# A block of four experts placed behind the wide pairs, five narrow pairs kept on the chip, and gathered rows added one pair sooner

## The chip, the cores and the metric

The kernel runs on one core of a Trainium2 chip. A core has five engines that run side by side, each through its own fixed list of instructions, in order: TensorE (PE) for matmuls and transposes, VectorE (DVE), ScalarE (ACT), GpSimd (POOL) and SyncE (SP). They wait for one another through semaphores. ACT, POOL and SP also issue transfers between the core's memory and the memory outside of it, which 16 DMA engines carry out. The metric is the time of one execution in microseconds (us) as the device counts it; less is better.

## The reference

One layer with three parts, in float32, on 256 tokens of 512 numbers: an attention block, a state-space block with a convolution, and a mixture of experts. The change touches the third part alone:

```python
scores = jax.nn.sigmoid(x @ gate_w)              # 256 tokens, 32 experts
topk_w, topk_i = jax.lax.top_k(scores, 6)
topk_w = topk_w / (jnp.sum(topk_w, axis=-1, keepdims=True) + 1e-20)
combine = jnp.sum(one_hot(topk_i, 32) * topk_w[..., None], axis=1)
g = jnp.einsum('td,edf->tef', x, wg)             # wg, wu: 32 x 512 x 192
u = jnp.einsum('td,edf->tef', x, wu)
routed = jnp.einsum('tef,efd,te->td', silu(g) * u, wd, combine)
shared = silu(x @ sg) * (x @ su) @ sd
return routed + shared
```

So each token goes through 6 of 32 experts, and the results are added with the token's weights. The layer's input is added on top, as after the other parts.

## The kernel before

Tokens stand in two token tiles of 128 (NT = 2). The attention and the state-space part come first and take the span up to about 839 us. The routing then ranks the experts: the first 8 (FIXED) stand as they are, the other 24 are sorted by how many tokens chose them. Sorted experts get 128 rows each down to position 18 (WIDE), and 64 rows behind that, except the four with the fewest tokens, which get 32 rows each and share one block of 128 rows, the block of four. A second path for the case that an expert has more tokens than rows stands behind a test on the device (`crowded`); it is not taken with these inputs.

Experts go in pairs, numbered n = 0 to 15. Pairs 0 to 8 are wide (two blocks of 128 rows), the narrow pairs hold two experts in one block, and the block of four takes two numbers. The loop at L1582 walks over `units`, all pairs but the second number of the block. Before, the order is: wide pairs 0 to 8, narrow pair 9, the block of four as 10 (11 is left out), narrow pairs 12 to 15. Two constants set this: SMALL = 20 is the place at which the block of four begins, and TAIL = 8 the number of experts behind it. FOUR is the block's unit, and LAST = 16 - TAIL/2 = 12 the first unit behind it.

One pass of the loop, for unit n:

- `gate_up` (L1484 for wide pairs, L1406 for narrow ones, L1439 for the block): the gate and up products on PE into the tile `ps_egu`, SiLU on ACT into `si`, and products on DVE into `hid` (L1495, L1416, L1450). The last of them is kept as `done[n]`.
- `fetch` (L1376): rows of a later unit are gathered from `xg` into `xg_sb` by a POOL transfer. `turn` (L1387) of the next unit: PE transposes into `xgTp` (L1392), a DVE copy to `xgT` (L1394). The next `gate_up` needs that copy.
- the down products of the unit before. Up to LAST, the result goes through an ACT copy to `y_sb`, and ACT issues its write to `ye` outside the core's memory (L1520, L1472, L1466). Behind LAST, `down_here` (L1474) keeps it in `y_sb`.
- for the units kept on the chip, `spread` (L1479): matmuls (L1482) with a matrix `spread` that carries each row to its token, with its weight, adding up in the PSUM tiles `total`, one per token tile.
- `load_pair`: POOL issues the three weight transfers of the pair six places on, into the buffers that the unit before has left (L1187).
- `turn_hidden` (L1421, L1498): PE transposes `hid` into `hidTp` for the down products.

The results in `ye` come back by `gather` (L1338): six POOL transfers per token tile, one for each chosen expert of a token, into `yk` tiles, and `add` (L1348) multiplies and adds them to `x_sb` on DVE (L1351), in a chain for each token tile. Experts that are kept on the chip have no row in `ye`; the gather reads a row of zeros for them. A gather waits for all the writes to `ye` before it. Token tile 0's gathers are written at LAST and take the six buffers of the pool `yp`; token tile 1's are written one unit later and take two buffers of the ring "xg" and then four of `yp`, which come free with the adds of token tile 0. `add_behind` (L1576) writes adds that may not stand ahead of `done[n]` on DVE: three behind pair 14's, nine behind pair 15's.

The matrix `spread` is made in `weights_back` (L1540), written in the pass of unit 3: for each token tile, eight scalings on DVE (L1560) into `pick`, four transposes on PE into a tile of the ring "x" of two (L1562), which `turn` uses too, and one copy (L1563).

At the end `finish` (L1623) adds `total` to `x_sb` on DVE, and SP stores the two tiles.

The order of instructions on each engine is not just the order of the program text. The framework's planner walks through the program before launch with costs of its own: when an engine is free by its reckoning, it takes the instruction that stands first in the text among those that are ready by its reckoning. `issue_after` holds instructions back behind a given one on their engine. On the chip each engine then keeps to the list that came out, whether or not the transfers are as quick as reckoned.

Of the kernel before, what the change touches and what calls it, by code (L numbers as in the profile page):

```python
# [11 lines left out]
FP = mybir.dt.float32  # L12
# [3 lines left out]
ALU = mybir.AluOpType  # L16
# [3 lines left out]
P = 128  # L20
# [29 lines left out]
TOPK = 6  # L50
FT = FSH // P
REST = FE - P
NP = NE // 2
# [4 lines left out]
WIDE = FIXED + 10  # L58
HALFP = P // 2
QUARTER = P // 4  # L60
SMALL = 20
HEAD = 4
TAIL = 8
NPL = 2 * (NE - FIXED) + (NE - WIDE) // 2 - (NE - WIDE) + (NE - FIXED) // 2
ZROW = WIDE * P + (SMALL - WIDE) * HALFP + 4 * QUARTER
NOROOM = 2 * NE * P
# [9 lines left out]
def perceiver_layer(ctx: ExitStack, tc: tile.TileContext, a: dict, out: bass.AP):  # L76
# [64 lines left out]
    def layer(ctx, bounded):  # L141
# [1196 lines left out]
        def gather(src, rows, t, rings):  # L1338

            got = []  # L1340
            for k, (pool, tag) in enumerate(rings):
                yk = pool.tile([P, DM], FP, tag=tag, name="yk")
                G.indirect_dma_start(out=yk, out_offset=None, in_=src,
                                     in_offset=bass.IndirectOffsetOnAxis(ap=rows[:, t, k:k + 1], axis=0))
                got.append(yk)
            return got
# [175 lines left out]
        with ExitStack() as rctx:  # L1522
            main = Rounds(rctx, weights)
            yp = rctx.enter_context(tc.tile_pool(name="yp", bufs=6))
            for k in range(KD):
                ps = main.ps_x.tile([P, HEAD * P], FP, tag="x", name="ps_pick")
                for t in range(NT):
                    TE.matmul(ps, xn[:, t, k * P:(k + 1) * P], pick[:, t].rearrange("p e r -> p (e r)"),
                              start=(t == 0), stop=(t == NT - 1))
                (S.copy if k % 2 else V.tensor_copy)(picked[:, k], ps.rearrange("p (e r) -> p e r", r=P))  # L1530
            for e in range(HEAD):
                main.xgT[e // 2, e % 2] = picked[:, :, e, :]


            idx, rowf, sc, rank, mask, iota = (m[n] for n in ("idx", "rowf", "gate", "rank", "mask", "iota"))
            result_rows()

            spread, = carve(m["kv", 0], (TAIL // 2, L))

            def weights_back():  # L1540

                V.tensor_tensor(sc, sc, mask, ALU.mult)
                V.tensor_tensor(sc, sc, m["den"].unsqueeze(2).to_broadcast([P, NT, NE]), ALU.mult)

                free = NE - FIXED
                V.tensor_tensor(member, m["at"].unsqueeze(1).to_broadcast([P, TAIL, NE]),
                                iota[:, free - TAIL:free].unsqueeze(2).to_broadcast([P, TAIL, NE]), ALU.is_equal)
                of, of_all = {}, carve(members, *[(TAIL,)] * 4)
                for t in range(NT):
                    for name, v in (("rank", rank), ("sc", sc)):  # L1550
                        V.tensor_tensor(own, member, v[:, t].unsqueeze(1).to_broadcast([P, TAIL, NE]), ALU.mult)
                        of[name, t] = of_all[len(of)]
                        V.tensor_reduce(of[name, t], own, AX.X, ALU.add)
                for t in range(NT):
                    tp = main.ps_x.tile([P, TAIL // 2, P], FP, tag="x", name="spreadT")
                    for u in range(TAIL // 2):
                        w = pick[:, t, u, :]
                        for i in range(2):
                            s = 2 * u + i
                            V.tensor_scalar(w[:, i * HALFP:(i + 1) * HALFP], iota[:, 0:HALFP], of["rank", t][:, s:s + 1],  # L1560
                                            of["sc", t][:, s:s + 1], ALU.is_equal, ALU.mult)
                        TE.transpose(tp[:, u, :], w, ident)  # L1562
                    V.tensor_copy(spread[:, :, t * P:(t + 1) * P], tp)  # L1563

            FIRST, LAST, FOUR = HEAD // 2, NP - TAIL // 2, SMALL // 2
            units = [n for n in range(NP) if n != FOUR + 1]
            gate_up = lambda n: (main.gate_up if 2 * n < WIDE else main.gate_up_quarters if n == FOUR else main.gate_up_halves)(n)
            turn_hidden = lambda n: (main.turn_hidden_halves if 2 * n >= WIDE and n != FOUR else main.turn_hidden)(n)
            down = lambda n: (main.down if 2 * n < WIDE else main.down_quarters if n == FOUR else main.down_halves)(n, ye)
            def spread_last(n, tiles=range(NT)):  # L1570
                main.spread(n, spread[:, n - LAST, :], total, n == LAST, n == NP - 1, tiles)

            fetched = set()
            got, r_x, r_k = [], [(main.e4, "xg")], [(yp, "yk")]

            def add_behind(n, k0, k1):  # L1576

                with tc.issue_after(main.done[n]):
                    for k in range(k0, k1):
                        add(got[k // TOPK], k // TOPK, [k % TOPK])  # L1580

            for u, n in enumerate(units):  # L1582
                before, coming = units[u - 1], units[u + 1:]
                gate_up(n)

                for f in coming[1:3 if n == LAST else 2]:
                    if FIRST <= f and f not in fetched:
                        main.fetch(f)
                        fetched.add(f)

                if FIRST < n + 1 and coming:
                    main.turn(coming[0])
                if 0 < n <= LAST:
                    down(before)
                    if n + 1 == FIRST:
                        main.turn(n + 1)
                elif n > LAST:
                    main.down_here(before)
                if n == LAST:
                    got.append(gather(ye, row_y, 0, r_k * TOPK))  # L1600
                elif n == LAST + 1:
                    total = [main.ps_ye.tile([P, DM], FP, tag="ye", name="total") for _ in range(NT)]
                    got.append(gather(ye, row_y, 1, r_x * 2 + r_k * 4))
                if n > LAST + 1:
                    spread_last(n - 2)
                if n == NP - 2:
                    add_behind(n, 0, 3)
                if n == NP - 1:
                    add_behind(n, 3, 2 * TOPK)
                for freed in range(before, n) if n > 0 else ():  # L1610
                    load_pair(freed + NHELD)
                if n == FIRST + 1:
                    weights_back()
                    some = nc.values_load(crowded, min_val=0, max_val=1)
                turn_hidden(n)

            spread_last(NP - 2, [0])
            main.down_here(NP - 1)
            spread_last(NP - 2, [1])
            spread_last(NP - 1)  # L1620

            def finish(t):
                V.tensor_tensor(x_sb[:, t, :], total[t], x_sb[:, t, :], ALU.add)  # L1623

            def store(t):
                nc.sync.dma_start(out[t * P:(t + 1) * P, :], x_sb[:, t, :])

            with tc.If(some == 0) as arms:
                for t in range(NT):
                    finish(t)  # L1630
                    store(t)
            with arms.Else():
                for t in range(NT):
                    finish(t)
                main.weights = {}
                for n in range(NP):
                    main.weights[n] = (held[2 * (n % 2)], held[2 * (n % 2) + 1], rests[n % 2])
                    load_weights(main.weights[n], n, True)
                    for h in range(NT):
                        r0 = [(2 * n + i) * L + h * P for i in range(2)]  # L1640
                        main.fetch(n, r0)
                        main.turn(n, 2)
                        main.gate_up(n)
                        main.turn_hidden(n)
                        main.down(n, ye2, r0)

                row2f, row2 = m["m8"][:, :, 0:TOPK], row_y
                V.tensor_scalar(rowf, rowf, float(NOROOM), float(NE * L), ALU.is_lt, ALU.mult)
                V.tensor_copy(row2f, row)
                V.tensor_tensor(row2f, row2f, rowf, ALU.add)  # L1650
                V.tensor_scalar(row2f, row2f, float(NE * L), None, ALU.min)
                V.tensor_copy(row2, row2f)
                for t in range(NT):
                    add(gather(ye2, row2, t, [(main.e4, "xg")] * TOPK), t)
                    store(t)
# [55 lines left out]
```

## Time and profile before

| | |
|---|---|
| median of 3 runs | 989.08 us (988.28 to 989.34) |
| the profiled execution's own time | 982.5 us |
| its span | 980.7 us |
| PE busy in the span | 956.7 us, 98% |
| first product of the expert stage | 843.3 us into the span |
| the block of four: gate and up begin | 930.4 us |
| end of PE's last matmul | 967.7 us |
| end of the last `add` and of the last `finish` on DVE | 969.1 and 970.4 us |

All times within the execution are in us from the start of the span. Busy times add up over an engine; PE's ends are modelled, and each float32 matmul shows as two instructions, each transpose as one. In an order of time a line gives the start, the length, engine and line, the operation, output and inputs with their shapes, and in brackets how long the engine idled before it and what ended that. L numbers are lines of the kernel.

### The profile page before, as it was taken

The page shows a single profiled execution, that of the slowest core. Times are in us where ns is not written, and L with a number is a line of the kernel's source. Part 1 is how long each engine was busy: PE and PEld are TensorE (multiplying, and loading weights), DVE is VectorE, ACT ScalarE, POOL GpSimd, SP SyncE. Part 2 cuts the span into 40 slices and gives each one's busy share as a digit, 9 for nine tenths or more (in the row PEclk, how much of TensorE's full clock was granted, in tenths as well). Part 3 has the DMA queues.
Part 4 walks back from the last instruction along what each step waited for, and adds up shares of the span by engine and source line. Part 5 has one row for each costly group of instructions (what it writes and reads, how often), then busy time and mean ns, then how long its engine had stood idle before and what let it go on. Part 6 is the DMA issues. An engine that isn't in the chain of part 4 may idle for free.

```text
span 980.7 us, 8874 instructions
## 1 busy us (share of the span) xinstructions
PE 956.7 (98%) x2725; PEld 451.6 (46%) x2725; DVE 497.4 (51%) x1013; ACT 386.9 (39%) x851; POOL 203.9 (21%) x212
## 2 busy tenths in 40 slices
PE   7999999999999999999999999999999999999994
PEld 3444444444444444444444444444465655455441
DVE  4456555454454544544545445358587656622133
ACT  3645444343443434434434344353153642122220
POOL 4443002001100200200200110000014233545432
PEclk9999999999999999999999999999999999999997
DMA  9735032122313304304113121150036353899973
GB/s 329 229 75 140 35 112 106 41 44 107 86 20 131 86 1 150 76 11 150 54 33 92 64 61 32 57 168 1 0 140 218 140 174 138 308 353 358 365 303 117
DMA packets 130940, 125.12 MB, mean 128 GB/s; under 512 B 80033, under 2 KB 99266, under 8 KB 125634
## 3 DMA queue, kind: packets, MB, share of 16 engines
q1 hardware_dynamic: 119216, 77.96, 26.4%
q0 software_dynamic: 7904, 40.90, 11.4%
q10 hardware_dynamic: 3762, 5.59, 1.6%
q8 instruction: 24, 0.39, 0.2%
q14 instruction: 34, 0.28, 0.1%
HBM read 88.76 MB, written 35.67 MB: 127 GB/s over the span
## 4 chain that ended last, share of the span: by engine, by line
PE 92%; issue 2%; DVE 2%; DMA 2%; POOL 1%; ACT 1%; SPq 0%; POOLq 0%; DVEq 0%
PE scT L571 23%; PE oT L596 23%; PE ps_kv L368 17%; PE ps_egu L222 5%; PE ps_self L222 4%; PE ps_v L222 2%; PE ps_o L794 2%; PE ps_ye L1512 2%; PE ps_k L222 2%; PE ps_xbc L222 1%; PE ps_out L988 1%; DMA yk<-ye,row_y 1%; PE ps_sgu L222 1%; PE ps_ye L1515 1%; PE xgTp L1392 1%
## 5 line engine op out<-in xcount | busy, mean ns | idle before, releaser
L587 DVE TENSOR_TENSOR lacc<-lacc,prT 128x512 f32<-128x512 f32 x256 | 182.8, 715 | 239.3 <-ACT prT L577 238.6
L577 ACT ACTIVATE prT<-scT,bq,rk 128x512 f32<-128x512 f32 x256 | 198.8, 777 | 254.3 <-PE scT L571 241.8
L571 PE MATMUL scT<-qT,kT 128*128 128x512 f32 x536 | 271.6, 593 | 0.0
L596 PE MATMUL oT<-prT,v 128*128 128x512 f32 x528 | 268.3, 592 | 0.0
L571 PEld LDWEIGHTS scT<-qT,kT 128*128 128x128 f32 x536 | 101.1, 190 | 124.8 <-issue 121.7
L596 PEld LDWEIGHTS oT<-prT,v 128*128 128x128 f32 x528 | 100.2, 190 | 125.8 <-issue 115.8
L200 POOL TENSOR_TENSOR rk<-pv,mhalf 128x4 f32<-128x4 f32 x32 | 32.3, 1010 | 369.3 <-DVE pv L199 369.3
L368 PE MATMUL ps_kv<-wkv,fast 128*128 128x512 f32 x112 | 53.4, 592 | 0.0
L258 ACT ACTIVATE sq<-kraw 128x128 f32<-128x128 f32 x128 | 35.6, 278 | 45.2 <-DVE kraw L386 43.1
L368 PE MATMUL ps_kv<-wkv,ctx 128*128 128x512 f32 x112 | 52.8, 592 | 0.0
L368 PE MATMUL ps_kv<-fast,fast 128*128 128x512 f32 x112 | 52.6, 592 | 0.0
L602 DVE TENSOR_TENSOR oacc<-oT,oacc 128x512 f32<-128x512 f32 x64 | 43.7, 683 | 0.0
L368 PEld LDWEIGHTS ps_kv<-wkv,fast 128*128 128x128 f32 x112 | 21.3, 190 | 26.8 <-issue 26.8
L368 PEld LDWEIGHTS ps_kv<-fast,fast 128*128 128x128 f32 x112 | 21.3, 190 | 26.8 <-issue 21.8
L368 PEld LDWEIGHTS ps_kv<-wkv,ctx 128*128 128x128 f32 x112 | 21.3, 190 | 26.8 <-issue 23.7
L362 POOL TENSOR_TENSOR fast<-ctx 128x512 f32<-128x512 f32 x7 | 9.4, 1336 | 113.0 <-PE ps_kv L368 94.2
L386 DVE TENSOR_TENSOR kraw<-ps_kv,fast 128x256 f32<-128x256 f32 x42 | 17.8, 424 | 28.2 <-PE ps_kv L368 28.2
L1495 DVE TENSOR_TENSOR hid<-si,ps_egu 128x128 f32<-128x128 f32 x18 | 5.2, 286 | 49.4 <-ACT si L1493 49.4
L794 PE MATMUL ps_o<-wo,qT 128*128 128x512 f32 x64 | 28.8, 592 | 0.0
L222 PE MATMUL ps_self<-wq,xT 128*128 128x512 f32 x64 | 28.1, 592 | 0.0
L607 DVE RECIPROCAL lacc<-ps_l 128x512 f32<-128x512 f32 x8 | 26.8, 3349 | 0.1
L368 PE MATMUL ps_kv<-fast,ctx 128*128 128x512 f32 x56 | 26.3, 592 | 0.0
(393 smaller groups left out, 1114.8 us busy)
## 6 DMA issues: line engine op xcount, KB each, us to landing
xg<-xn SPq DMA_DIRECT2D x6, 2560.0 KB, 9.3
ctx<-in_ctxT_dram SPq DMA_DIRECT2D x7, 1024.0 KB, 5.4
kd<-tr SPq DMA_DIRECT2D x112, 64.0 KB, 2.4
kT<-kd SPq DMA_DIRECT2D x28, 256.0 KB, 2.8
ye<-y_sb ACTq DMA_DIRECT2D x20, 256.0 KB, 8.1
wq<-in_wq_dram SPq DMA_DIRECT2D x4, 1024.0 KB, 14.2
wo<-in_wo_dram SPq DMA_DIRECT2D x4, 1024.0 KB, 10.5
w_in<-in_W_inT_dram SPq DMA_DIRECT2D x4, 1024.0 KB, 5.7
```

Of the source, the lines that this page charges most:

```text
L200: return G.tensor_tensor(dst, v[:, :n], mhalf[:, :n], ALU.pow)
L222: TE.matmul(ps, lhs(k), rhs_of(k), start=(k == 0), stop=(k == KD - 1))
L258: S.activation(sq[:, h, :], raw[:, h, :], AF.Square, accum_out=ss[:, h:h + 1])
L368: TE.matmul(ps, lhs(k), rhs(k), start=(start and k == 0), stop=(k == 1), skip_group_check=True)
L571: scored.append(TE.matmul(sc, kT[:, g, i * P:(i + 1) * P], qT[:, t, heads4(g), :].rearrange("p h q -> p (h q)"), start=True, stop=True).ins)
L577: S.activation(pr, sc, AF.Exp, bias=shift, scale=SCALE if r is None else r[:, i, g:g + 1])
L587: V.tensor_tensor(la, la, pr, ALU.add)
L596: TE.matmul(outs[g, t], v[:, i, g * HD:(g + 1) * HD], pr, start=(n == 0), stop=last)
L602: V.tensor_tensor(ov, outs.pop((g, t)), ov, ALU.add)
L607: V.reciprocal(rl, ps)
L794: TE.matmul(m["ps_o", t], aT[:, t, h, :], wo[j][:, h % 4, :], start=(h == 0), stop=(h == NH - 1))
L1512: TE.matmul(ps[i], h[:, i, :], wd[i], start=True, stop=False)
```

## The change

The block of four moves one unit ahead, to directly behind the wide pairs. SMALL becomes 18 and TAIL 10, so the order is: wide pairs 0 to 8, the block of four as 9 (10 is left out), narrow pairs 11 to 15. LAST becomes 11. All five narrow pairs stand behind the block, and all of them keep their results on the chip; nineteen blocks are written to `ye` where there were twenty. `spread` has five blocks per token tile in place of four: `weights_back` makes them in two tiles of the ring "x" per token tile, four and one, and the fifth block uses the first slot of `pick` again. Token tile 0's gathers are written at unit 11 and token tile 1's at unit 12; the latter now take first four buffers of `yp` and then two of the ring "xg". At LAST the rows of three later units are fetched in place of two. Six adds are written behind pair 13's last product, four behind pair 14's and two behind pair 15's.

```diff
-SMALL = 20
+SMALL = 18
 HEAD = 4
-TAIL = 8
+TAIL = 10
...
                 for t in range(NT):
-                    tp = main.ps_x.tile([P, TAIL // 2, P], FP, tag="x", name="spreadT")
-                    for u in range(TAIL // 2):
-                        w = pick[:, t, u, :]
-                        for i in range(2):
-                            s = 2 * u + i
-                            V.tensor_scalar(w[:, i * HALFP:(i + 1) * HALFP], iota[:, 0:HALFP], of["rank", t][:, s:s + 1],
-                                            of["sc", t][:, s:s + 1], ALU.is_equal, ALU.mult)
-                        TE.transpose(tp[:, u, :], w, ident)
-                    V.tensor_copy(spread[:, :, t * P:(t + 1) * P], tp)
+                    for u0 in range(0, TAIL // 2, HEAD):
+                        us = range(u0, min(u0 + HEAD, TAIL // 2))
+                        tp = main.ps_x.tile([P, HEAD, P], FP, tag="x", name="spreadT")
+                        for u in us:
+                            w = pick[:, t, u - u0, :]
+                            for i in range(2):
+                                s = 2 * u + i
+                                V.tensor_scalar(w[:, i * HALFP:(i + 1) * HALFP], iota[:, 0:HALFP], of["rank", t][:, s:s + 1],
+                                                of["sc", t][:, s:s + 1], ALU.is_equal, ALU.mult)
+                            TE.transpose(tp[:, u - u0, :], w, ident)
+                        V.tensor_copy(spread[:, u0:us[-1] + 1, t * P:(t + 1) * P], tp[:, 0:len(us)])
...
-                for f in coming[1:3 if n == LAST else 2]:
+                for f in coming[1:4 if n == LAST else 2]:
...
-                    got.append(gather(ye, row_y, 1, r_x * 2 + r_k * 4))
+                    got.append(gather(ye, row_y, 1, r_k * 4 + r_x * 2))
                 if n > LAST + 1:
                     spread_last(n - 2)
-                if n == NP - 2:
-                    add_behind(n, 0, 3)
-                if n == NP - 1:
-                    add_behind(n, 3, 2 * TOPK)
+                if n >= NP - 3:
+                    add_behind(n, *{NP - 3: (0, TOPK), NP - 2: (TOPK, 2 * TOPK - 2), NP - 1: (2 * TOPK - 2, 2 * TOPK)}[n])
```

## The prediction

> **What bounds the kernel now.** The page's busy times first: TensorE (PE) is busy 98% of the span, so work taken off any other engine gains only where PE is not last.
>
> ```profile
> PE 956.7 (98%) x2725; PEld 451.6 (46%) x2725; DVE 497.4 (51%) x1013; ACT 386.9 (39%) x851; POOL 203.9 (21%) x212
> DMA  9735032122313304304113121150036353899973
> ```
>
> The diff touches only the expert stage, from 839 us on, so next the busy times in stretches of it (columns: stretch, length, busy us and count of PE, PEld, DVE, ACT, POOL, then clock, DMA share, GB/s):
>
> ```profile
> 930.00:940.00 10.00, 10.00 (x77) 4.08 (x75) 2.41 (x10) 3.07 (x7) 5.35 (x6) 1.00 1.02 411
> 940.00:950.00 10.00, 10.00 (x54) 4.13 (x48) 2.00 (x5) 2.05 (x5) 0.33 (x1) 1.00 0.73 302
> 950.00:960.00 10.00, 10.00 (x45) 3.94 (x42) 4.83 (x11) 1.62 (x4) 7.87 (x8) 1.00 0.62 164
> 960.00:970.00 10.00, 7.68 (x21) 2.67 (x19) 6.67 (x11) 1.54 (x3) 4.33 (x5) 1.00 0.53 157
> ```
>
> PE never idles before its last matmul, the DMA engines are full until about 947 and then half free, DVE is mostly idle. Third, the end, in the orders of time of ACT, POOL, PE and DVE:
>
> ```profile
> 943.03 0.33 ACTq L1466 DMA_DIRECT2D ye<-y_sb  x1
> 949.67 0.95 POOL L1343 DMA_INDIRECT yk<-ye,row_y  x1 [9.95 <-issue]
> 956.40 1.15 POOL L1343 DMA_INDIRECT yk<-ye,row_y  x1 [0.30 <-issue]
> 964.52 1.02 POOL L1343 DMA_INDIRECT yk<-ye,row_y  x1 [0.30 <-issue]
> 964.85 2.82 PE L1482 MATMUL total<-y_sb,xc 128*128 128x512 f32 x6
> ...
> 951.34 0.29 DVE L1416 TENSOR_TENSOR hid<-si,ps_egu 128x128 f32<-128x128 f32 x1 [4.21 <-ACT si L1414]
> 951.54 0.46 DVE L1419 TENSOR_TENSOR hid<-si,ps_egu 64x64 f32<-64x64 f32 x2
> 952.03 0.69 DVE L1394 COPY xgT<-xgTp 128x512 f32<-128x512 f32 x1
> 952.93 0.75 DVE L1351 SCALAR_TENSOR_TENSOR x_sb<-yk,lacc,x_sb 128x512 f32<-128x512 f32 x1 [0.20 <-DMA yk<-ye,row_y]
> 954.52 0.75 DVE L1351 SCALAR_TENSOR_TENSOR x_sb<-yk,lacc,x_sb 128x512 f32<-128x512 f32 x1 [0.84 <-DMA yk<-ye,row_y]
> 955.97 0.75 DVE L1351 SCALAR_TENSOR_TENSOR x_sb<-yk,lacc,x_sb 128x512 f32<-128x512 f32 x1 [0.70 <-DMA yk<-ye,row_y]
> 958.70 0.29 DVE L1416 TENSOR_TENSOR hid<-si,ps_egu 128x128 f32<-128x128 f32 x1 [1.98 <-ACT si L1414]
> ...
> 968.34 0.75 DVE L1351 SCALAR_TENSOR_TENSOR x_sb<-yk,lacc,x_sb 128x512 f32<-128x512 f32 x1 [0.65 <-DMA yk<-ye,row_y]
> 969.12 1.29 DVE L1623 TENSOR_TENSOR x_sb<-total,x_sb 128x512 f32<-128x512 f32 x2
> ```
>
> Two chains race. PE ends at 964.85 + 2.82 = 967.67. The block of four writes its result at 943.03, the first gather leaves at 949.67, the twelfth at 964.52, and its add ends at 969.09. The gathers lose by 1.4 us, and the two final adds end at 970.41, 20.74 us behind the first gather. Quicker gathers alone can gain no more than the way from there to PE's end, less than 2 us. Mark the three adds: DVE reached each 0.2 to 0.8 us before its rows had landed, and what stood behind them (the products "hid" of the last pair) escaped only because they were not ready before 958.7. Last, the issue-to-landing times for short windows around single issues, the block's write and the sixth gather:
>
> ```profile
> ye<-y_sb ACTq DMA_DIRECT2D x1, 256.0 KB, 5.7
> yk<-ye,row_y POOLq DMA_INDIRECT x1, 4.9
> ```
>
> The same view gives 8.1 for the write at 936.47 and 7.6 to 10.6 for those of 905 to 932, while weights fill the DMA engines. The gathers' landings in order: 3.2, 3.4, 3.7, 3.9, 4.4, 4.9, 4.1.
>
> **The change, part by part.**
>
> *PE work.* One more pair is spread over both token tiles. One pair's spread is four L1482 instructions, which hold PE from 953.41 to 955.13: +1.72. Two more L1562 transposes: eight took 1.02, so +0.26. Products and down matmuls are the same, in another order. PE is never idle, so these 1.98 lie on its path: it would end at 969.65. The first total is ready two instructions ahead of that, so only the second final add (0.68, and 0.04 from PE's end to its reader) is left behind PE: 970.37, against 970.41. Without any wait the change is worth nothing.
>
> *The fifth block of the spread (third pair).* It reuses a `pick` slot, so its two DVE scalings (0.3 each) wait for PE's first transpose, and four PSUM tiles go through two slots. If PE finds nothing else, that is about 1 us per token tile, 2 in all; if products of the next pair fill it, nothing; a gain is excluded, since nothing is removed. I take 0: before, PE passed this place without a gap and eight products of the next pair stand right behind. DVE gains nine wider reductions and products (+0.1 each on 0.42), four scalings and two copies (0.3 each), 2.7 us; it idles over 7 of 10 us from 850 to 880, which hides it. Without that cover it would delay a "hid", at most by those 2.7.
>
> *The block one unit sooner.* It needs the weights of pair index 10 at 924 instead of 930; they were issued at 895.62 to 898.12 and take about 10 us, so 16 us of room. Its write moves: its down matmuls start where pair 9's started (933.75, plus 0.26, plus 0.11 for turning three hidden blocks instead of two: 934.12) instead of at 939.39, so the write leaves at 937.76 instead of 943.03. There the weights are still moving: I take 8.1 us (nearest in time and load; bounds 5.7 and 10.6), so it lands at 945.86. Before, the first gather left 0.94 behind the landing: now 946.80, 2.9 sooner and not 5.3. One write of 256 KB fewer: nothing, PE waits for no transfer. The last pair's row fetch now comes a unit sooner on POOL, ahead of the last weights; POOL idles 3.2 us there, so nothing, else 1.25 us on weights with 8 us of room.
>
> *The adds.* All six of token tile 0 may now stand on DVE behind the hidden products of pair 13, and they are written ahead of pair 14's. The order on an engine is fixed ahead of launch, and before, all three allowed adds stood in front of the next pair's products though their rows came late. I take it that the same happens with six. The sixth gather leaves 6.73 behind the first and takes 4.9: its rows are there at 946.80 + 11.63 = 958.43, add done 959.18. Behind it queue pair 14's products (0.69, as 951.34 to 952.03) and the copy of pair 15's turned rows (0.69): 960.56. PE needs that copy for pair 15's gate and up, which began at 955.44 and, 1.98 later, would begin at 957.42. It begins at 960.6 instead: a stall of 3.2. From there PE's rest is as before: 967.67 + 5.16 = 972.83. Token tile 1's rows land by 965.4, so PE decides and the final adds end 0.72 behind it: 973.55, against 970.41. Sum: +3.1.
>
> *The slots.* Token tile 1's first four gathers now wait for adds 0 to 3, not its last four; by the offsets of before the earliest leaves at 955.0 and add 0 ends at 950.8, so nothing; if the adds were late, the gathers would be as late.
>
> Against the profiled execution's own 982.5 (a span of 980.7 and 1.8 around it): 985.6. The median of the runs, 989.08, is 6.6 longer than that execution, and no row shows where those 6.6 lie; I add the same 3.1 to it: 992.2.
>
> *A rule against this.* The write's 8.1 us stands in a row. The Trainium skill (DMA: Bandwidth & Descriptors, Queues, rings and completion order) says that each DMA engine goes round between the queues that have work, a packet from each, so a write on ACT's queue should not stand behind the weights on POOL's. By that rule the time is rival 3's. The rows of 7.6 to 10.6 do not look like it, though no run here shows the packets' order.
>
> **Rivals.**
>
> 1. *No stall; not slower.* The order puts pair 14's products behind at most four adds. The fourth add ends at 946.80 + 7.66 + 0.75 = 955.2, products and copy follow by 956.6, ahead of PE's nominal 957.42; the fifth add is the point from which it decides. Then the final adds end at 970.37: 0.0, 989.0. For it: the planner may reckon the gathers late. Against: it reckoned three of them early before, and pair 14's products are ready only at 953.3 now, which leaves room for more adds ahead of them.
> 2. *Five ahead.* Fifth rows at 946.80 + 9.54 = 956.34, copy done 958.5, a stall of 1.1: +1.0, 990.1.
> 3. *The write gets through at once.* With half of 410 GB/s its 256 KB take 1.3 us on top of the 2.6 that the stores of the output need: landing 941.7, first gather 942.6, sixth add done 955.0: no stall, 989.0. For: the 5.7 of the last write. Against: the writes at 7.6 and more.
> 4. *More gain.* If the 6.6 us that the runs are longer lie in transfers, the gathers lose by more than 1.4 there; each us later adds one to the gain, up to 2.9 where no add stalls PE: 986.2. It needs 2 us of lateness to pass 0.2%.
> 5. *Later still.* The write takes 10.6 (2.5 more), or the fifth block stalls PE for its 2 us: 994.2 to 994.7.
>
> **How the numbers follow.** Forecast 0.50, rival 1 0.12, rival 2 0.10, rival 3 0.04, rival 4 0.11, rival 5 0.13. A measurement of this kernel tells about 0.2% (2 us) from no change. Slower: the forecast, rival 5 and 0.01 of rival 2, 0.64; same: rivals 1 and 3 and the rest of 2, 0.25; faster: rival 4, 0.11. The range leaves out rival 4's outer part and what lies beyond rival 5: 987.6 to 995.2. The forecast alone spans a write of 7.6 to 9.6: 991.7 to 993.7.
>
> **What would show it.** In the changed profile: the first gather near 946.8; six adds without a "hid" between them, DVE waiting for gathered rows in front of most; a PE gap of about 3 us ahead of the last pair's products; twenty "total" instructions instead of sixteen; no DVE wait at the end but for PE's totals. It is wrong if a "hid" stands among the first five adds, or the first gather leaves before 943 or after 949.

## The result, and the profile after

The changed kernel takes 986.8 us (median of 20 runs, 984.95 to 988.7) against 988.14 (20 runs, 987.01 to 989.69): a ratio of 0.9985, 95% interval 0.9979 to 0.9992. That is 1.3 to 1.5 us less, inside the 0.2% named as the bound, but clear of zero. The forecast was 3.1 us more, in a range of 987.6 to 995.2: the measured time lies below it, and the sign is the other one. The profiled execution of after took 986.18, with a span of 984.5.

The page of after, busy times of PE and the DMA row in 40 slices:

```profile
PE 961.5 (98%) x2731; PEld 453.0 (46%) x2731; DVE 499.5 (51%) x1019; ACT 386.9 (39%) x851; POOL 205.0 (21%) x212
DMA  9735042122313304304214111250046452799983
```

PE has six instructions more, the four spreads and two transposes of the sum. Busy times in stretches, in the columns of before:

```profile
940.00:950.00 10.00, 10.00 (x52) 4.19 (x50) 1.84 (x5) 2.05 (x5) 1.87 (x2) 1.00 1.03 425
950.00:960.00 10.00, 10.00 (x47) 4.02 (x44) 4.33 (x8) 1.62 (x4) 7.05 (x7) 1.00 0.64 206
960.00:970.00 10.00, 9.26 (x34) 3.58 (x33) 6.20 (x13) 1.88 (x4) 7.51 (x7) 1.00 0.63 183
970.00:980.00 10.00, 6.08 (x17) 1.93 (x15) 2.97 (x5) 0.96 (x2) 0.00 (x0) 1.00 0.27 84
```

PE works 6.08 us beyond 970 where before it had ended at 967.7. The orders of time of ACT, POOL, PE and DVE at the end:

```profile
942.86 0.33 ACTq L1466 DMA_DIRECT2D ye<-y_sb  x1
...
951.12 0.95 POOL L1343 DMA_INDIRECT yk<-ye,row_y  x1 [8.39 <-issue]
...
958.09 0.95 POOL L1343 DMA_INDIRECT yk<-ye,row_y  x1 [0.30 <-issue]
959.34 1.03 POOL L1187 DMA_INDIRECT v<-in_down_rest_dram,place  x1 [0.30 <-issue]
...
967.92 1.42 POOL L1343 DMA_INDIRECT yk<-ye,row_y  x1 [0.30 <-issue]
...
962.76 0.69 PE L1425 MATMUL hidTp<-ident,hid 128*128 128x128 f32 x2 [0.31 <-DVE hid L1416]
963.84 0.54 PE L1412 MATMUL ps_egu<-wkv,xgT 128*64 128x384 f32 x1 [0.40 <-DVE xgT L1394]
...
973.25 2.82 PE L1482 MATMUL total<-y_sb,xc 128*128 128x512 f32 x6
...
951.87 0.69 DVE L1394 COPY xgT<-xgTp 128x512 f32<-128x512 f32 x1
954.59 0.75 DVE L1351 SCALAR_TENSOR_TENSOR x_sb<-yk,lacc,x_sb 128x512 f32<-128x512 f32 x1 [2.03 <-DMA yk<-ye,row_y]
...
961.75 0.75 DVE L1351 SCALAR_TENSOR_TENSOR x_sb<-yk,lacc,x_sb 128x512 f32<-128x512 f32 x1 [0.76 <-DMA yk<-ye,row_y]
962.42 0.28 DVE L1416 TENSOR_TENSOR hid<-si,ps_egu 128x128 f32<-128x128 f32 x1
...
963.09 0.69 DVE L1394 COPY xgT<-xgTp 128x512 f32<-128x512 f32 x1
...
975.32 1.48 DVE L1623 TENSOR_TENSOR x_sb<-total,x_sb 128x512 f32<-128x512 f32 x2 [2.70 <-PE total L1482]
```

Nearly all that the prediction described is there: the six adds in a row with no "hid" between them, DVE waiting for rows ahead of most of them, a gap on PE (0.31 and 0.40, so smaller than the 3 us forecast), PE's totals last. DVE ends at 976.80, 6.4 us later than in the first execution of before (970.41). Yet that span is only 3.8 us longer, and the timed runs are shorter. From DVE's last instruction to the end of the span it is 10.3 us in before and 7.7 in after. So the end of the span does not follow the end of PE and DVE one to one.

What does follow? The closing instructions of each engine's queue, in the view of the line that closes the program (columns: count, shortest/median/longest in ns, first and last start). Before, then after:

```profile
L1707 POOLq DRAIN  x3: 40/107/6512, 973.4 to 980.5; - x3
L1707 SPq DRAIN  x3: 7/7/130, 974.8 to 980.2; - x3
...
L1707 DVEq DRAIN  x2: 10/34/58, 972.2 to 980.2; - x2
```

```profile
L1707 POOLq DRAIN  x3: 40/107/6512, 976.5 to 984.2; - x3
L1707 SPq DRAIN  x3: 7/7/131, 981.9 to 983.9; - x3
...
L1707 DVEq DRAIN  x2: 10/42/73, 980.7 to 983.9; - x2
```

POOL's first closing drain lasts 6.51 us; no other engine's lasts over 0.13. In before it starts at 973.4, ends at 979.9, and the span ends at 980.7. SP, which stores the output, has been at its own drain since 974.8. In after POOL's starts at 976.5, 7.3 us ahead of 983.8, and SP's at 981.9. What leads to POOL's drain stands in the view of the branch behind the last gathers, in before:

```profile
L1628 POOLq COMPARE_BRANCH  x2: 34/38/41, 960.5 to 970.3; - x2
L1628 POOLq INC_SWDGE_SEM  x1: 1747/1747/1747, 968.5 to 968.5; - x1
```

The last gather leaves at 964.52 and its rows land at 968.24; POOL waits for them, spends 1.75 us on that semaphore instruction, branches at 970.3 and is at its drain at 973.4: 8.9 us from the last gather to the drain.

### The profile page after: what moved, and what is told of

Its sections match the earlier page's. It is cut to its first block, busy times and chain, and to the rows that moved or that the text cites. A ratio compares the mean times of both kernels' runs of the same rounds, so it can differ in the third digit from the quotient of the medians.

```text
span 984.5 us, 8893 instructions
## 1 busy us (share of the span) xinstructions
PE 961.5 (98%) x2731; PEld 453.0 (46%) x2731; DVE 499.5 (51%) x1019; ACT 386.9 (39%) x851; POOL 205.0 (21%) x212
## 4 chain that ended last, share of the span: by engine, by line
PE 92%; DVE 3%; issue 2%; ACT 1%; DMA 1%; POOL 1%; SPq 0%; DVEq 0%; POOLq 0%
PE scT L571 23%; PE oT L596 23%; PE ps_kv L368 17%; PE ps_egu L222 4%; PE ps_self L222 3%; PE ps_v L222 2%; PE ps_o L794 2%; PE ps_ye L1512 2%; PE ps_k L222 2%; PE ps_xbc L222 1%; PE ps_out L988 1%; PE ps_sgu L222 1%; PE ps_ye L1515 1%; PE xgTp L1392 1%; PE ps_yd L928 1%
## 5 line engine op out<-in xcount | busy, mean ns | idle before, releaser
L571 PEld LDWEIGHTS scT<-qT,kT 128*128 128x128 f32 x536 | 101.1, 190 | 124.9 <-issue 121.7
L596 PEld LDWEIGHTS oT<-prT,v 128*128 128x128 f32 x528 | 100.2, 190 | 125.8 <-issue 115.8
```

The costliest lines, as they stand in the source:

```text
L571: scored.append(TE.matmul(sc, kT[:, g, i * P:(i + 1) * P], qT[:, t, heads4(g), :].rearrange("p h q -> p (h q)"), start=True, stop=True).ins)
L596: TE.matmul(outs[g, t], v[:, i, g * HD:(g + 1) * HD], pr, start=(n == 0), stop=last)
```

## The experiments

The first question was whether the profiled execution of before, shorter than all its timed runs, was an unusual one, and whether the early adds cost or gain. So both kernels were profiled again, and one part of the change was undone.

> The kernel before, once more, for a second profile. Theory A (the profiled execution of before was a lucky one at the start of the expert stage): this one lasts about 988 us, 5 to 6 us longer than the first profile's 982.5; ACT and DVE stand idle for some us without a cause between 843 and 852, as they did in the profile after (the first SiLU of the stage at 850.1, not 846.5), and PE stops there for 2 to 6 us; from the first product behind that to the end nothing differs from the first profile by more than 1 us. Rival B (the lucky place was the end): the start of the stage looks as in the first profile, and the 5 to 6 us lie between the write of the block of four and the final adds, with gathers that land later.

> A third profile of the kernel before, to see how much of it differs from execution to execution. Theory A: the stop at the start of the expert stage is there again, between 2 and 7 us, and the end is the same within 1 us. Rival B: the end differs by several us and the start does not.

> The changed kernel, once more. Theory A: about 986.8 us; a stop of 2 to 4 us at the start of the expert stage as in its first profile; six adds of gathered rows ahead of pair 14's products again, with a PE stop of about 1 us behind them. Rival B: the same start and an end that differs by several us.

Measured: 984.86 and 986.48 for before (spans 983.1, 984.6), 986.26 for after (984.4). Theory A holds on the place: the start of the stage differs, and from the first SiLU to PE's end before takes 121.7, 121.7 and 121.2 us. It does not hold on the size: about 988 was expected of the first, and it took 984.9. The first SiLU of the expert stage ran at 846.0 in the first execution of before, at 849.0 and 849.7 in these, and at 850.1 and 850.0 in after. ACT's order of time, after and then (from a later series) after again:

```profile
843.84 0.59 ACT L1530 COPY xc<-ps_pick 128x512 f32<-128x512 f32 x1 [3.54 <-PE ps_pick L1528]
850.10 0.55 ACT L1493 ACTIVATE si<-ps_egu 128x192 f32<-128x192 f32 x2 [5.68 <-PE ps_egu L222]
```

```profile
844.27 0.59 ACT L1530 COPY xc<-ps_pick 128x512 f32<-128x512 f32 x1 [3.55 <-PE ps_pick L1528]
846.91 0.33 ACT L1493 ACTIVATE si<-ps_egu 128x192 f32<-128x192 f32 x1 [2.05 <-PE ps_egu L222]
```

In some executions ACT and, with gaps of 0.3 to 1.4 us for which the profile names no other engine, DVE stop there; ACT idles 4.9 to 5.7 us in place of 2.1, some 2.8 to 3.7 us more, and then does two SiLUs close to one another. Both kernels have it. The three series of this section ran on three chips. All eight profiles of the first two show the stop, none of the four of the third does, so it may go with the chip and not with the single execution; nothing here separates the two. In four of the profiles with the stop (after, its variant with the transfer moved ahead, and both variants of before, below) the granted clock of PE falls to 0.50 to 0.54 for 2 us or more behind it, between 852 and 858; in the others it stays at 1.00. All this shifts what follows, so times below are compared from the first SiLU on, or by the runs of one series.

Undone: the early adds.

```diff
-                if n >= NP - 3:
-                    add_behind(n, *{NP - 3: (0, TOPK), NP - 2: (TOPK, 2 * TOPK - 2), NP - 1: (2 * TOPK - 2, 2 * TOPK)}[n])
+                if n == NP - 2:
+                    add_behind(n, 0, 3)
+                if n == NP - 1:
+                    add_behind(n, 3, 2 * TOPK)
```

> The changed kernel with its adds where they were before: three behind pair 14's products, nine behind pair 15's. Nothing but DVE's order differs. If the six early adds cost what the changed profile shows (PE's last gate and up 1.2 us late, and the last products behind four more adds), this one is 1 to 2 us faster than the changed kernel, 985 to 986 us. If the early adds are what gains, as their place one pair sooner would have it, it is slower than the changed kernel by 1 us or more: the last adds would then end behind PE.

Measured: 987.69 (12 runs) against 987.28 for before, ratio 1.0005 (0.9995 to 1.0014). So without the early adds nothing is left of the gain; by the ratios this is 2.0 us slower than after, as the second alternative had it, but not for its reason: the last add ends at 975.4, ahead of PE. Why it is slower, its profile does not settle. POOL's order of time, then ACT's and PE's:

```profile
964.63 0.94 POOL L1343 DMA_INDIRECT yk<-ye,row_y  x1 [0.30 <-issue]
969.43 1.21 POOL L1343 DMA_INDIRECT yk<-ye,row_y  x1 [3.86 <-DVE x_sb L1351]
...
964.22 0.59 ACT L1477 COPY y_sb<-ps_ye 128x512 f32<-128x512 f32 x1 [6.02 <-PE ps_egu L1412]
967.10 0.37 ACT L1427 COPY hidT<-hidTp 128x256 f32<-128x256 f32 x1 [2.29 <-remote]
...
967.52 0.87 PE L1434 MATMUL ps_ye<-w_in,hidT 128*64 128x512 f32 x1 [3.36 <-ACT hidT L1427]
```

The twelfth gather waits 3.9 us for the fourth add to free its buffer, which stands behind the last pair's products. But ACT does nothing here from 958.2 to 967.1 except one copy, which itself runs 4.7 us behind the end of its product on PE (959.49), and the profile names no cause. So the last pair's SiLU runs at 967.37 though its products were done at 964.16, its "hid" is as late, and PE idles 3.4 us for `hidT`. In no other profile does ACT fall as far behind PE in this stretch. The stop is in the gather's wait and in PE's end (978.82, 2.7 us behind after's) alike. This execution, the longest but two of the twelve, does not say what the late adds alone cost.

Which end counts is what the next two runs were for. In the one, DVE's closing sums in before are made longer; in the other, POOL gets two more gathers whose rows nobody reads.

```diff
-                V.tensor_tensor(x_sb[:, t, :], total[t], x_sb[:, t, :], ALU.add)
+                for op, a0, b0 in ((ALU.add, total[t], x_sb[:, t, :]), (ALU.subtract, x_sb[:, t, :], total[t]), (ALU.add, total[t], x_sb[:, t, :])): V.tensor_tensor(x_sb[:, t, :], a0, b0, op)
```

> The kernel of before, in which each of the two closing sums on VectorE is done three times (add, subtract, add), so that the output's rows leave some 2.7 us later (four extra instructions of 0.65 to 0.7 us). Theory C (the end belongs to POOL: the span ends 12.5 us after the rows of the last gather have landed, and the output's landing lies some 5 us ahead of the end of POOL's closing drain): no change, within 0.4 us of before. Rival R (the end belongs to PE and DVE, as the prediction had it): slower by 2.4 to 2.8 us. In the profile C expects the time from DVE's last instruction to the span's end to shrink from 10.2 us to about 7.5, and R expects it to stay at 10.2.

```diff
-                    got.append(gather(ye, row_y, 1, r_x * 2 + r_k * 4))
+                    got.append(gather(ye, row_y, 1, r_x * 2 + r_k * 4) + gather(ye, row_y, 1, r_k * 2))
```

> The kernel of before with two more gathers behind the twelfth on POOL; they fetch rows that nobody reads, so PE, DVE and the output are not held by them. Theory C: slower by two gathers of 0.95 to 1.4 us with 0.3 between them, 2.5 to 3.4 us. Rival R (PE and DVE set the end): no change, within 0.4 us.

Measured, beside 988.46 for before in that series: 988.2 with the longer sums, ratio 0.9992 (0.9982 to 1.0003), and 991.89 with the two gathers, ratio 1.0030 (1.0019 to 1.0042), 3.0 us by the ratio and 3.4 by the medians. Both as theory C had it and neither as rival R. The end of the first, DVE's order of time and the closing view:

```profile
976.01 1.29 DVE L1623 TENSOR_TENSOR x_sb<-total,x_sb 128x512 f32<-128x512 f32 x2
977.21 1.28 DVE L1623 TENSOR_TENSOR x_sb<-x_sb,total 128x512 f32<-128x512 f32 x2
978.40 1.28 DVE L1623 TENSOR_TENSOR x_sb<-total,x_sb 128x512 f32<-128x512 f32 x2
```

```profile
L1707 POOLq DRAIN  x3: 40/107/6512, 979.9 to 987.0; - x3
L1707 SPq DRAIN  x3: 7/7/130, 984.8 to 986.7; - x3
```

Some 2.4 us of work were put on the very end of the chain that the prediction took for the path (979.68 against 977.30), and the span still ends 7.3 us behind the start of POOL's drain. DVE's end to the span's end shrank to 7.5. It used up the room, though: SP came to its drain at 984.8. In the second, POOL's drain starts at 981.9, SP's at 980.8, and the span ends at 989.5; POOL's drain is 0.16 us longer there (6.675).

In the same series went two variants of after, meant to move each of the two ends alone.

```diff
-                    add_behind(n, *{NP - 3: (0, TOPK), NP - 2: (TOPK, 2 * TOPK - 2), NP - 1: (2 * TOPK - 2, 2 * TOPK)}[n])
+                    add_behind(n, *{NP - 3: (0, 4), NP - 2: (4, 2 * TOPK - 2), NP - 1: (2 * TOPK - 2, 2 * TOPK)}[n])
```

> The kernel of after with four of the adds behind pair 13 instead of six, the fifth and the sixth behind pair 14; the gathers and all else are as in after. The hidden products of pair 14 then come some 1.3 to 2.9 us sooner, and PE's and DVE's end with them, by 1.2 to 2.5 us. Theory C: the time stays that of after within 0.5 us (986.3 to 987.3 where before stands at 988), because the last gather leaves no sooner. Rival R: 1.2 to 2.5 us faster than after.

Measured: 986.54, ratio to before 0.9980 (0.9969 to 0.9991), not to be told from after's 0.9985. But the run does not decide: PE's end did not move (976.36 against 976.07). The products of pair 14 came at 959.59 instead of 962.42. Then six adds stood in front of pair 15's products; DVE waited 3.33 us for the rows of the second of them and 0.38 for those of the last, from the tenth gather, and the products came at 969.03 (969.45 in after). The stall went to the next pair.

```diff
-                if n == LAST:
+                for freed in range(before, n) if n > 0 else ():
+                    load_pair(freed + NHELD)
+                if n == LAST:
                     got.append(gather(ye, row_y, 0, r_k * TOPK))
...
-                for freed in range(before, n) if n > 0 else ():
-                    load_pair(freed + NHELD)
```

> The kernel of after with the transfer of pair 15's shared weights, which stands behind the sixth gather, issued ahead of the first gather, in the 8 us in which POOL waits for the last write of results. Nothing else moves. Theory C: the six gathers behind it leave one issue (1.0 us and 0.3) sooner, so 1 to 1.4 us faster than after, less where the output's landing, which in after lies 1.1 us ahead of POOL's end, takes over. Rival R: no change against after within 0.4 us, as PE and DVE wait for that transfer in neither kernel.

Measured: 986.21, ratio 0.9978 (0.9963 to 0.9993), by the ratios 0.7 us under after, within the intervals of both; so this run decides between C and R no more than the one before. The gathers take 15.3 us from the first to the twelfth instead of 16.8, and POOL's drain starts 2.1 us sooner than in after (974.4); the span, at 983.6, is 0.9 shorter. It now ends 9.2 us behind the drain's start: another chain has taken over. With four adds behind pair 13 that distance is 8.9, in after 8.0.

So theory C needs a second chain. Over all fourteen profiles the span ends either 7.3 us behind the start of POOL's drain (7.5 with the two gathers more), or 2.0 to 2.6 us behind SP's first closing drain, whichever is later. This rule was read off the profiles, and the last series is its only test. SP's first drain itself starts 3.4 to 4.3 us behind SP's branch at the end of the stores; whether the landing of the output or the closing instructions' own arrival sets this I did not separate, and where the expectations speak of the output's landing, it is this drain that was read. By this rule before has 3.1 to 3.5 us of room (2.4 behind SP's drain, in its three profiles) on the side of PE, DVE and SP, and after has none. The last series asked that of after:

```diff
-                V.tensor_tensor(x_sb[:, t, :], total[t], x_sb[:, t, :], ALU.add)
+                for op, a0, b0 in ((ALU.add, total[t], x_sb[:, t, :]), (ALU.subtract, x_sb[:, t, :], total[t]), (ALU.add, total[t], x_sb[:, t, :])): V.tensor_tensor(x_sb[:, t, :], a0, b0, op)
```

> The kernel of after with each closing sum done three times, the same 2.7 us as in the run on before. Theory C2 (two chains meet at the end: POOL's, whose closing drain starts 8.5 us after the last gather was issued and which ends 7.3 us after that start, and the output's, which ends 2 to 2.5 us after its rows have landed; in before POOL's is the later by 3.1 to 3.5 us, in after the output's is the later by about 0.6): slower than after by 2.4 to 2.9 us, where the same edit cost before nothing. Plain theory C (POOL alone): slower by 0 to 1.6 us.

```diff
-                    got.append(gather(ye, row_y, 1, r_k * 4 + r_x * 2))
+                    got.append(gather(ye, row_y, 1, r_k * 4 + r_x * 2) + gather(ye, row_y, 1, r_k * 2))
```

> The kernel of after with two more gathers behind the twelfth, whose rows nobody reads. Theory C2: they cost 2.5 to 3.4 us of POOL, of which 0.6 lies beside the output's landing: slower than after by 1.8 to 2.8 us. Rival R (PE and DVE alone): no change against after.

> The kernel of after once more, for comparison in the same series: 1 to 2 us faster than before, as in its first series (986.8 against 988.1), by every theory.

This series, on another chip, ran at a lower level: before 983.7 (27 runs), after 982.2 (11 runs), ratio 0.9981 (0.9972 to 0.9990), the same gain as at first. The longer sums gave 984.01, 1.8 us over after by the medians and 2.2 by the ratios, where on before they cost nothing. That lies between what plain C allows and C2's 2.4 to 2.9, and with intervals of 1 us either way the time does not tell them apart. The profile does: POOL's drain would allow an end at 978.8, and the span ends at 981.4, 2.3 us behind SP's. In it SP's first drain comes 1.9 us later, counted from the first SiLU (133.0 against 131.1): the added sums took 2.4, and PE ended 0.4 sooner in that execution. The two gathers gave 985.99, 3.8 us over after by the medians and 3.4 by the ratios, more than the 1.8 to 2.8 expected. In the one execution that was profiled POOL took 4.4 us from its branch (972.9) to its drain (977.3), where all others took 2.5 to 3.1. Why, and whether the other runs have it, is open. Both edits cost something on after, as they must where both chains are near the end; the sizes were missed both times.

Last, both chains of after made shorter together: the transfer ahead of the gathers, and four adds behind each of the three pairs.

```diff
-                    add_behind(n, *{NP - 3: (0, TOPK), NP - 2: (TOPK, 2 * TOPK - 2), NP - 1: (2 * TOPK - 2, 2 * TOPK)}[n])
+                    add_behind(n, *{NP - 3: (0, 4), NP - 2: (4, 8), NP - 1: (8, 2 * TOPK)}[n])
```

> Both chains of after made shorter: the transfer of pair 15's shared weights ahead of the first gather (as in the run that did only this), and four adds behind the hidden products of each of the pairs 13, 14 and 15, where after has six, four and two. Theory C2: POOL's chain ends 2 us sooner than in after (about 981.7 instead of 983.8), the output's 1 to 2 us sooner, as the products of the last pair no longer wait for the adds in front; so 1 to 2 us faster than after and 2.3 to 3.5 us faster than before. Plain theory C: 1.5 to 2 us faster than after, as POOL alone decides. Rival R: 1 to 2 us faster than after too, so this run does not tell R apart; it shows what the two together are worth.

Measured: 979.96 (5 runs, 979.05 to 981.91), ratio to before 0.9957 (0.9944 to 0.9971), 3.7 us by the medians; 2.2 us under after, a little more than expected of either. It beats both kernels. The profiled execution is the longest of the five. DVE's order of time and the closing view:

```profile
955.84 0.75 DVE L1351 SCALAR_TENSOR_TENSOR x_sb<-yk,lacc,x_sb 128x512 f32<-128x512 f32 x1 [0.54 <-DMA yk<-ye,row_y]
956.51 0.28 DVE L1416 TENSOR_TENSOR hid<-si,ps_egu 128x128 f32<-128x128 f32 x1
...
962.49 0.75 DVE L1351 SCALAR_TENSOR_TENSOR x_sb<-yk,lacc,x_sb 128x512 f32<-128x512 f32 x1 [1.59 <-DMA yk<-ye,row_y]
963.16 0.28 DVE L1416 TENSOR_TENSOR hid<-si,ps_egu 128x128 f32<-128x128 f32 x1
...
971.17 1.48 DVE L1623 TENSOR_TENSOR x_sb<-total,x_sb 128x512 f32<-128x512 f32 x2 [3.77 <-PE total L1482]
```

```profile
L1707 POOLq DRAIN  x3: 40/107/6512, 971.2 to 979.8; - x3
L1707 SPq DRAIN  x3: 7/7/130, 977.7 to 979.5; - x3
```

The products of pair 14 follow the fourth add, at 956.51, and no longer the sixth; no gap is left on PE behind the start of the stage; POOL's drain would allow an end at 978.5, and SP's sets 980.1.

## Why the prediction was wrong

Three profiled executions without the stop at the start of the stage, in us from the first SiLU (846.00, 846.91, 848.05):

| | before | after | the last variant |
|---|---|---|---|
| first gather | 103.7 | 100.6 | 100.2 |
| twelfth gather | 118.5 | 117.3 | 114.6 |
| PE's end | 121.7 | 125.5 | 123.9 |
| DVE's end | 124.4 | 126.2 | 124.6 |
| POOL's drain starts | 127.4 | 125.9 | 123.2 |
| SP's first drain | 128.8 | 131.1 | 129.7 |
| end of the span | 134.7 | 133.5 | 132.1 |
| POOL's drain + 7.3 | 134.7 | 133.2 | 130.5 |
| SP's drain + 2.4 | 131.2 | 133.5 | 132.1 |

*The step that failed* is the last one: "so PE decides and the final adds end 0.72 behind it: 973.55, against 970.41. Sum: +3.1". It carries the end of DVE one to one into the time. In before nothing there decides, by 3.1 to 3.5 us: 2.4 us more on DVE cost nothing, two gathers that nobody waits for cost 3.0. The first mistake is already in the reading of before, "two chains race", with the gathers losing to PE at the final adds. There was a third, from the last gather's landing through POOL's closing: the gathers come last at the final adds by 1.4 us, and at the end of the span by over 3. The chain of waits on the page does not show it, as it ends at DVE's last sum. The prediction took the time from there to the end of the span, 10.3 us, as fixed: it is 10.1 to 10.3 in the three profiles of before, but 7.5 with the longer sums, 13.2 with the two gathers, and 7.3 to 7.7 in after. For the same reason "quicker gathers alone can gain no more than the way from there to PE's end" and "without any wait the change is worth nothing" were wrong: a sooner twelfth gather is worth what it gains until SP's side takes over.

*PE's work.* Six more instructions, as counted; in the table's profiles the spread's 1.72 came as forecast, and ten transposes took 1.43 where eight had taken 1.02, +0.41 for +0.26. Their cost fell into the room.

*The fifth block.* Taken as 0 in bounds of 0 to 2; PE shows 0.29 us ahead of a transpose in after, 1.02 and 0.96 in two other executions, and no gap over 0.15 in the rest. Not on the path until the room is used.

*The block one unit sooner.* Right: the first gather leaves 3.1 us sooner in the table, forecast 2.9. Rival 3 fell, and with it the rule put against the change: the Trainium skill (DMA: Bandwidth & Descriptors, Queues, rings and completion order) has the engines go round between queues by packets. By rival 3's estimate the write should then land in some 4 us. In after the first gather leaves 8.26 us behind the write's issue, with the DMA engines full (1.03 from 940 to 950), and where the landing can be read, in the table's profile of after, it is 7.7 us; the prediction took 8.1. The trace does not show that rule at work.

*What was missed on POOL.* "POOL idles 3.2 us there, so nothing" looked at the row fetch only. The transfer of pair 15's shared weights slipped between the sixth and the seventh gather (1.03 and 0.30 us), and gathers beside DVE's adds took up to 1.42 us to issue instead of 0.95 (in before up to 1.35). So the twelve gathers take 16.7 us instead of 14.9 in the table's profiles; of these 1.8 us the transfer makes 1.4 and the longer issues 0.3. Of the 3.1 us only 1.3 reach the twelfth. That is about the measured gain.

*The adds.* The order was as forecast, six in front of pair 14's products. The stall was mis-sized: 0.7 to 1.0 us of idle PE in the three profiles of after instead of 3.2. In the first of them the sixth add began 3.7 us behind the issue of its gather, not 4.9, and PE came to the place later. DVE's end moved by 1.8 us in the table, not 3.1; even the right size, carried into the time, would have given the wrong sign. The early adds cost PE this and are needed all the same: without them the gain is gone. That this is for the twelfth gather's wait for a buffer is likely but not shown, as the one profile of it has the stop of ACT.

*The slots.* "Nothing" held for after, where no gather waits for an add.

*Rival 4* gave the right sign for nearly the right place: the gathers were worth more than the race at the final adds allowed. Its reason was another: the runs' longer time was not in the gathers, as the twelfth leaves 117.9 and 119.1 us behind the first SiLU in the two profiles of before with the stop and 118.5 in the one without. Those two spans are 2.4 and 3.9 us longer than the first; where the rest of the 6.6 lies is open. The level as such explains nothing of the difference: at 988 and at 983.7 the gain is the same.

## What to carry to other kernels

Ask where the span really ends: read the closing instructions of every queue, POOL's too, before the time behind the last compute instruction is taken as fixed. Here three executions of before gave it alike, so repeating the profile would not have shown it; making each end longer by itself did. A kernel whose last transfers are issued by POOL may end with POOL's closing, and then the last such transfer's place counts, with slack for everything else; a transfer that can go ahead of a wait then costs that chain nothing (the twelve gathers took 15.3 us with it moved, 16.8 without). When a stall is moved from one pair to the next nothing is won, so adds that wait for rows go in front of products only as far as their rows are there in time.

## What the runs showed of the hardware

POOL's closing drain grew from 6.512 to 6.675 us when two gathers were added (6.676 on after), and its semaphore instruction from 1.747 to 1.787: 0.08 and 0.02 us for each transfer that POOL issues. If that line holds, the 76 indirect transfers of POOL in before (36 of weights, 16 of rows, 12 of rows to `xg`, 12 gathers) make up 6.2 of the 6.5 us, by this estimate; two points are all there is. The Trainium skill (VectorE: DVE Perf Modes, The DRAIN you can't avoid) gives the drains of the runtime's start and end as some 12 ns on all five engines. Whether the closing drains here, which stand on a line of the kernel (L1707), are of that kind no run shows. DVE's, of 10 to 73 ns, are of that order; POOL's first is not, and the measurement decides.

From POOL's last branch to its drain it takes 2.5 to 3.1 us in all profiles but one (4.4); in before three packets of the instruction queue q14 and one of q8 arrive in that stretch (970.3 to 973.4). The Trainium skill (Runtime: NRT & Kernel Launch, Instruction fetch mechanics) says that a branch out of the fetched window makes the engine wait for a fetch. The trace fits it here but does not show it: the packets do not tell which engine they are for, and SP branches in the same stretch (971.4). Whether the stop of ACT and DVE at 843 to 850 is of that kind was not tried; its cause stays open.

A gather issued while DVE runs an add of gathered rows takes longer to issue. Over all fourteen profiles, the 56 gathers with no such add running beside them took 0.94 to 0.95 us each, DVE's other instructions notwithstanding; the 116 with one took 0.94 to 1.46, half of them over 1.1.
